# Router logits of a mixture of experts: four token tiles at once on TensorE's four column groups

## The chip, the core and the metric

The kernel runs on one core of one Trainium2 chip. The metric is the device time of one execution in microseconds (us). The engines named below are TensorE (PE; PEld is its weight load), VectorE (DVE), ScalarE (ACT), GpSimd (POOL) and SyncE (SP, which here only issues DMAs).

## The reference, cut to what matters

Two layers on 2048 tokens of 512 features. The first is a long convolution (an attention without softmax): products of keys and values are convolved with a kernel per head group and combined with the normalised queries. The second is a mixture of 16 experts. The change touches the second layer's router: logits of each token for 16 experts, and the choice of the four largest.

```python
x = x + xattn(ctx_2048, ctx_2048, layernorm(x), ssm_kernel, D, 8)
h = layernorm(x)                                # (T, 512), T = 2048
scores = softmax(h @ gate_w.T)                  # gate_w (16, 512)
topk_w, topk_i = top_k(scores, 4)
topk_w = topk_w / (topk_w.sum(-1) + 1e-20)
# each expert takes its first 256 tokens, in order of token
eout = (silu(xg @ w_gate) * (xg @ w_up)) @ w_down * weight
out = x + scatter_add(eout) + (silu(h @ sw_gate) * (h @ sw_up)) @ sw_down
```

All of it is in float32; one float32 matmul instruction of the program appears in the trace as two passes of TensorE, each a weight load and a MATMUL (a transpose appears as one).

## The kernel before

The 2048 tokens are 16 tiles of 128. The order of the instructions on every engine is the order in which the program issues them[...].

**The loop of the first layer** (line 645, 16 rounds, in the order 1, 0, 2, 3, ... of `seq`) computes one token tile of the convolution in a round. A round has four calls of `attend` (line 441), two for each of its two heads: TensorE convolves into `y` (lines 455 to 476; in all but the first ones a part `shared` comes first, which ScalarE copies to `again`), VectorE combines `y` with the queries through `z` (lines 478 to 504) into `f` (line 505), and GpSimd adds up `f` into `oT` (lines 506 to 509). `y` has two buffers. GpSimd makes the products `kv` for the next tile (line 425).

**Work of the second layer lies between.** When a tile is done, `add_to_x` (line 512) transposes it and adds it to `xs`; its statistics and normalisation run on ScalarE and GpSimd, and the transposed tile `xnT` comes either through DRAM (`send_blocks`, `fetch_blocks`, and a transpose in 32x32 blocks on VectorE, line 391) or, for the first and last tiles, through TensorE and a copy of ScalarE (line 721). Most tiles are ready two rounds after their convolution (`ready(n - 2)`, line 713, just before the fourth `attend`), the first and last one round after (line 723).

`ready` (line 629) calls `by_feature` (line 536): four matmuls with `xnT[:, c, n, :]` (128x128) as stationary and `gwT[:, c, :]` (128x16) as moving operand give `lg`, 128 tokens by 16 experts; VectorE copies it to `logits` and chooses (lines 543 to 552): the eight largest (`tops`), a memset of places 4 to 7, a match-and-replace into `rest`, and `sel`, one where an expert is chosen. `count` (line 637) adds `sel` on GpSimd to the running number `early`. `gwT` is made once, in round 0 (lines 693 to 696).

`ready` also appends a generator of the shared expert (`shared_block`, line 129) to the list `behind`; `fill(n)` (line 618) issues its next n pieces. These pieces are matmuls `sgt`, `sgu` and `so` that stand between the parts of the convolution.

**Buffers of the accumulator memory.** The pool `ps_tr` holds two buffers under the one tag `pt`. They go in turn to the transposes of `transpose_in` and `add_to_x`, to `shared`, to `lg`, and to `pg`: each new one waits until the one before the last has been read.

**After the loop** (lines 734 to 745) the last tile goes the same way, with `fill` between. Then positions within each expert's list are computed from `sel` and `early` (line 777), `compare` and `find` (lines 807 and 818) make the token lists of the experts, and the expert loop (line 979) gathers, computes and adds by DMA.

**Constants.** `masks` (line 188) makes index tables on GpSimd and VectorE in rounds 6 to 8; `exch` (line 261) is a 128x128 table that `begin` (line 288) uses in round 0 and nothing uses later.

Of the kernel before, what the change touches and what calls it, by code (L numbers as in the profile page):

```python
# [52 lines left out]
def ssm_attention__then__moe_kernel(  # L53
# [22 lines left out]
    nc = tc.nc  # L76
# [4 lines left out]
    const = ctx.enter_context(tc.tile_pool(name="const", bufs=1))  # L81
# [16 lines left out]

    xs = keep.tile([P, NT, L], F32, name="xs")
    xnT = keep.tile([P, NC, NT, P], F32, name="xnT")  # L100
    gwT = keep.tile([P, NC, E], F32, name="gwT")
    logits = keep.tile([P, NT, E], F32, name="logits")
    tops = keep.tile([P, NT, 8], F32, name="tops")
    sel = keep.tile([P, NT, E], BF16, name="sel")
# [83 lines left out]
    def masks():  # L188

        col_i = const.tile([P, R, B], I32, name="col_i")
        col_b = const.tile([P, P], F32, name="col_b")
        par_i = const.tile([P, 1], I32, name="par_i")
        bat_i = const.tile([P, 1], I32, name="bat_i")
        row_i = const.tile([P, 1], I32, name="row_i")
        par_b = const.tile([P, 1], F32, name="par_b")
        nc.gpsimd.iota(col_i, pattern=[[0, R], [1, B]], base=0, channel_multiplier=0)
        nc.gpsimd.iota(par_i, pattern=[[0, 1]], base=0, channel_multiplier=1)  # L200
        slot_i = const.tile([P, P], I32, name="slot_i")
        slot_f = const.tile([P, P], F32, name="slot_f")
        nc.gpsimd.iota(slot_i, pattern=[[1, P]], base=0, channel_multiplier=0)
        nc.gpsimd.tensor_copy(slot_f, slot_i)

        tok_i = const.tile([P, NT, 3], I32, name="tok_i")
        tok_f = const.tile([P, NT, 3], F32, name="tok_f")
        tok = const.tile([P, NT, 3], BF16, name="tok")
        row_f = const.tile([P, 1], F32, name="row_f")
        nc.gpsimd.memset(tok_i, 1)  # L210
        nc.gpsimd.iota(tok_i[:, :, 1], pattern=[[R, NT]], base=0, channel_multiplier=0)

        empty_i = const.tile([P, NSL], I32, name="empty_i")
        empty = const.tile([P, NSL], F32, name="empty")
# [27 lines left out]
        masked.update(tri=tri, tri_b=tri_b, same_b=same_b, slot_f=slot_f, tok=tok, empty=empty)  # L242
        yield
# [3 lines left out]
    with ExitStack() as att:  # L247
# [141 lines left out]
        def transpose_blocks(dst, got):  # L389

            nc.vector.transpose(dst, got.rearrange("p j (c f) -> p c j f", f=BK))
# [141 lines left out]
        def store(n, xn):  # L533
            nc.sync.dma_start(out=by_tile(xw_d[0:T, 0:L])[n], in_=xn)

        def by_feature(n):

            lg = ps_tr.tile([P, E], F32, name="lg", tag="pt")
            for c in range(NC):
                nc.tensor.matmul(  # L540
                    lg, lhsT=xnT[:, c, n, :], rhs=gwT[:, c, :], start=(c == 0), stop=(c == NC - 1)
                )
            nc.vector.tensor_copy(logits[:, n, :], lg)

            top = tops[:, n, :]
            nc.vector.max(out=top, in_=logits[:, n, :])
            nc.vector.memset(tops[:, n, K:8], 3.0e38)
            rest = small.tile([P, E], F32, name="rest")
            nc.vector.match_replace(
                out=rest, in_to_replace=top, in_values=logits[:, n, :], imm_value=-3.0e38  # L550
            )
            nc.vector.tensor_tensor(sel[:, n, :], rest, logits[:, n, :], ALU.is_lt)

        toeps = {}

# [72 lines left out]

        def ready(n):

            by_feature(seq[n])
            for t in range(2) if n == 1 else range(n, n + (n > 0)):
                count(t)
            if n < 4 or n + 1 == sum(blocks_left[0]):
                behind.append(shared_block(*blocks_left.pop(0)))

        def count(t):

            nc.gpsimd.tensor_add(early[:, t + 1, :], early[:, t, :], sel[:, t, :])

        nc.gpsimd.memset(early[:, 0, :], 0.0)
        making = masks()
# [2 lines left out]
        for n in range(NT):  # L645
# [16 lines left out]
                kvs.append(products(t * HT + 1, 1, k2))  # L662
            if n - 2 in MILD:
                transpose_blocks(xnT[:, :, n - 2, :], got_x)
            if more and not swift and n:
                qn = load.tile([P, L], F32, name="qn", tag="kn")
                stats = statistics(qn, xs[:, seq[n + 1], :])
# [24 lines left out]
            if n == 0:  # L692
                pg = ps_tr.tile([P, NC, P], F32, name="pg", tag="pt")
                for c in range(NC):
                    nc.tensor.transpose(pg[:, c, 0:E], gw[:, c * P : (c + 1) * P], ident[:E, :E])
                nc.scalar.copy(gwT, pg[:, :, 0:E])
            fill(2)
            if n > 0:
                normalise(xn, xs[:, seq[n - 1], :], *xstats)
# [13 lines left out]
                ready(n - 2)  # L713

            attend(t * HT + 1, 1, 2, tps[1], kvs[1], q2, oT)
            if n == 0:
                windows()
            if n - 1 in MILD:
# [323 lines left out]
```

## Time and profile before

| | us |
|---|---|
| three runs | 702.88, 705.42, 707.62; median 705.42 |
| the profiled execution, its own time | 702.86 |
| its span, from first to last instruction | 701.1 |
| TensorE busy / weight load busy | 675.0 (96%) / 510.0 (73%) |
| VectorE / ScalarE / GpSimd busy | 365.1 / 196.1 / 305.8 |
| logit matmuls, line 540: MATMUL / LDWEIGHTS | 15.5 / 16.7 in 128 passes |

The start takes until about 41 us, the loop of the first layer until about 348, the tail, the rest of the shared expert and the lists until about 430, the experts until about 686; the last additions to the output end the span.

How to read the profile's views. A row of the page over 40 slices gives the busy share in tenths for each 17.5 us. The view by windows gives busy time and, in brackets, the number of instructions of each engine in a stretch. The timeline lists one engine's instructions in order of time: start, duration, line, operation, tiles (out<-in), shapes, count; in square brackets the idle time ahead of it and what ended it. The chain of waits is followed back from the last instruction: at each step to what released it, or to the instruction before it on its engine. Durations of a pass are longer than the distance between passes, because passes overlap; the distance is what counts.

### The profile page before, as it was taken

Reading aid. Unit: us, or ns where it says so; the run is one execution under the profiler, and the core shown is the slowest. Engines: PE = TensorE matmul, PEld = TensorE weight load, DVE = VectorE, ACT = ScalarE, POOL = GpSimd, SP = SyncE. Lnnn points to the kernel's source line nnn. Section 1 sums busy time; section 2 is a strip of 40 time slices with the busy share of each in tenths; the row PEclk is TensorE's granted clock in tenths of the full one; section 3 lists DMA queues with packets and bytes.
Section 4 is the critical chain, followed back from the end, with each engine's and each line's share of the span. In section 5 each row is a group of like instructions: output and inputs, shape, how many; then the busy total and the mean of one; then the engine's idle time right before and its main releaser. Section 6 shows DMA issues by size and latency. Waiting matters only on the chain.

```text
span 701.1 us, 9862 instructions
## 1 busy us (share of the span) xinstructions
PE 675.0 (96%) x3437; PEld 510.0 (73%) x3437; DVE 365.1 (52%) x845; ACT 196.1 (28%) x501; POOL 305.8 (44%) x478
## 2 busy tenths in 40 slices
PE   6889999899999999999999999999999999999994
PEld 5677887777877877877868686777777777777772
DVE  4946666778968677675635311333333344333221
ACT  3443423444342343421212011122221111221220
POOL 6666646777765576545200200222233333222221
PEclk9999999999999999999999999999999999999998
DMA  6783546656566646441028301677776777777632
GB/s 156 233 238 91 137 129 148 176 135 165 146 158 172 166 105 151 123 117 45 16 90 265 88 12 34 184 211 208 202 200 186 199 199 206 203 194 194 186 46 30
DMA packets 90929, 104.17 MB, mean 149 GB/s; under 512 B 10416, under 2 KB 63504, under 8 KB 90880
## 3 DMA queue, kind: packets, MB, share of 16 engines
q1 hardware_dynamic: 83424, 86.24, 43.9%
q0 software_dynamic: 7168, 17.04, 11.6%
q8 instruction: 27, 0.44, 0.3%
q10 hardware_dynamic: 288, 0.26, 0.2%
q14 instruction: 22, 0.18, 0.1%
HBM read 75.86 MB, written 27.66 MB: 148 GB/s over the span
## 4 chain that ended last, share of the span: by engine, by line
PE 90%; DMA 5%; DVE 2%; issue 1%; SPq 1%; ACT 0%; POOLq 0%; ACTq 0%; DVEq 0%
PE sgu L155 20%; PE y L455 16%; PE pgu L918 16%; PE eo L960 12%; PE so L172 12%; PE pgu L938 4%; PE pt L126 2%; PE pgu L930 2%; PE shared L455 2%; PE sgt L141 2%; PE lg L540 1%; DMA swt<-in_L_ffn_sw_up 1%; DMA got<-sent 1%; PE ip L823 1%; PE pt L516 1%
## 5 line engine op out<-in xcount | busy, mean ns | idle before, releaser
L455 PE MATMUL y<-kv,toep 128*128 128x288 f32 x528 | 138.6, 407 | 2.7 <-DVE f L505 1.9
L455 PEld LDWEIGHTS y<-kv,toep 128*128 128x128 f32 x528 | 99.1, 190 | 33.1 <-issue 6.3
L918 PE MATMUL pgu<-xgT,w 128*128 128x256 f32 (+1 forms) x544 | 113.8, 367 | 0.8 <-ACT xgT L890 0.8
L918 PEld LDWEIGHTS pgu<-xgT,w 128*128 128x128 f32 x544 | 98.6, 190 | 20.4 <-issue 7.7
L969 POOL DMA_INDIRECT out<-eo_sb,idx x32 | 51.1, 1596 | 107.4 <-DMA out<-eo_sb,idx 71.7
L877 POOL DMA_INDIRECT g<-xw_d,idx x32 | 32.0, 1001 | 139.7 <-PE eo L960 60.4
L507 POOL TENSOR_TENSOR f<-f 128x256 f32<-128x256 f32 x60 | 43.7, 729 | 98.7 <-DVE f L505 93.3
L960 PE MATMUL eo<-wd,mid 128*128 128x512 f32 (+1 forms) x192 | 86.4, 598 | 0.0
L432 POOL TENSOR_TENSOR kv<-k 128x256 f32<-128x256 f32 x128 | 86.1, 704 | 0.0
L155 PE MATMUL sgu<-xnT,swg 128*128 128x256 f32 (+1 forms) x400 | 78.1, 338 | 1.8 <-DVE tail L149 1.8
L155 PE MATMUL sgu<-xnT,swu 128*128 128x256 f32 (+1 forms) x400 | 77.8, 337 | 0.0
L172 PE MATMUL so<-swd,smid 128*128 128x512 f32 x160 | 74.4, 594 | 0.0
L155 PEld LDWEIGHTS sgu<-xnT,swg 128*128 128x128 f32 x400 | 65.3, 191 | 9.1 <-DVE tail L149 2.0
L155 PEld LDWEIGHTS sgu<-xnT,swu 128*128 128x128 f32 x400 | 64.7, 191 | 6.3
L960 PEld LDWEIGHTS eo<-wd,mid 128*128 128x128 f32 (+1 forms) x192 | 35.1, 190 | 37.9 <-issue 33.6
L925 ACT ACTIVATE eact<-pgu 128x256 f32<-128x256 f32 (+1 forms) x34 | 12.6, 372 | 152.0 <-PE pgu L918 152.0
L172 PEld LDWEIGHTS so<-swd,smid 128*128 128x128 f32 x160 | 29.7, 190 | 31.0 <-issue 29.4
L164 ACT ACTIVATE act<-sgu 128x256 f32<-128x256 f32 (+1 forms) x50 | 17.1, 341 | 122.1 <-PE sgu L155 122.1
L926 DVE TENSOR_TENSOR mid<-eact,pgu 128x256 f32<-128x256 f32 (+1 forms) x34 | 13.8, 405 | 70.8 <-ACT eact L925 70.8
L478 DVE TENSOR_TENSOR y<-y,again 128x576 f32<-128x576 f32 x28 | 21.4, 766 | 53.1 <-PE y L455 50.3
L968 DVE TENSOR_SCALAR eo_sb<-eo,g 128x512 f32<-128x512 f32 x32 | 24.0, 750 | 46.3 <-PE eo L960 46.3
L505 DVE TENSOR_TENSOR f<-y,z 128x512 f32<-128x512 f32 x64 | 44.3, 692 | 6.2
(164 smaller groups left out, 859.0 us busy)
## 6 DMA issues: line engine op xcount, KB each, us to landing
w<-in_L_ffn_w_gate SPq DMA_DIRECT2D x16, 704.0 KB, 4.4
w<-in_L_ffn_w_up SPq DMA_DIRECT2D x16, 704.0 KB
got<-sent SPq DMA_DIRECT2D x36, 256.0 KB, 6.2
toep<-win_d SPq DMA_DIRECT2D x28, 320.0 KB, 5.2
wd<-in_L_ffn_w_down SPq DMA_DIRECT2D x16, 512.0 KB, 5.0
xs<-in_x SPq DMA_DIRECT2D x16, 256.0 KB, 5.8
kn<-in_ctx SPq DMA_DIRECT2D x16, 256.0 KB, 6.2
xw_d<-xn SPq DMA_DIRECT2D x16, 256.0 KB, 2.9
```

The costliest lines, as they stand in the source:

```text
L155: nc.tensor.matmul(pgu[:, k, :], lhsT=sw[:, c, f * P : (f + 1) * P], rhs=toks[:, c, :], start=(c == 0), stop=(c == NC - 1),)
L172: nc.tensor.matmul(po, lhsT=m[:, i * P : (i + 1) * P], rhs=swd[:, (f - 1) % (NF + 1), :], start=(f == 0), stop=(f == NF),)
L432: nc.gpsimd.tensor_mul(kv[:, c, 0 : ND * HB].rearrange("p (d w) -> p d w", d=ND), kh[:, c, 0:HB].unsqueeze(1).broadcast_to([P, ND, HB]), v ...
L455: nc.tensor.matmul(out, lhsT=toep[:, m * P : (m + 1) * P], rhs=rhs, start=(n == 0), stop=(n == len(pairs) - 1),)
L505: nc.vector.tensor_add(f, yd, z[:, :, :, BACK : BACK + HB])
L507: adder.tensor_add(f[:, :, 0:2, :], f[:, :, 0:2, :], f[:, :, 2:4, :])
L877: nc.gpsimd.indirect_dma_start(out=g, out_offset=None, in_=xw_d[:, :], in_offset=bass.IndirectOffsetOnAxis(ap=idx[:, e, n : n + 1], axis=0),)
L918: nc.tensor.matmul(pgu[:, k, cols], lhsT=w[:, k, c, f * P : (f + 1) * P], rhs=xgT[:, c, cols], start=(c == 0), stop=(c == NC - 1),)
L938: nc.tensor.matmul(pgu[:, 0, cols], lhsT=wt[:, c, 0:P], rhs=xgT[:, c, cols], start=(c == 0), stop=(c == NC - 1),)
L960: nc.tensor.matmul(po, lhsT=mid[:m, f, n * P : (n + 1) * P], rhs=wd[:m, f, :], start=(f == 0), stop=(f == NI - 1),)
L968: nc.vector.tensor_scalar_mul(o, po, g[:, L + e : L + e + 1])
L969: nc.gpsimd.indirect_dma_start(out=out, out_offset=bass.IndirectOffsetOnAxis(ap=idx[:, e, n : n + 1], axis=0), in_=o, in_offset=None, comp ...
```

## The change

The logits of four tiles are computed together, when the last of the four is ready (after tiles 3, 7, 11, and after tile 14 for three tiles; tile 15 alone as before). Operands are exchanged: the stationary operand is now `gwT`, 32 columns wide, of which 16 hold the gate's weights and 16 are zero; the moving operand is `xnT`. Each tile's result goes to its own 32 partitions of the one buffer `lq`[...]: the result is expert by token. ScalarE copies `lq` into `exch`, whose old content is no longer needed. After the fourth `attend` of that round, `turn_logits` transposes the copy by TensorE in one piece (`lt`), and VectorE copies 16 of every 32 columns to `logits`. `choose` then handles one tile each time it is called, twice a round: after the first `attend` and at the round's end. Its operations are the old ones, and the addition to `early` is now among them.

`gwT` is wider and is cleared once by GpSimd at the start. In `masks`, `slot_i` takes the memory of `col_i`, and two index operations change places for that.

```diff
-    gwT = keep.tile([P, NC, E], F32, name="gwT")
+    gwT = keep.tile([P, NC, BK], F32, name="gwT")
+    nc.gpsimd.memset(gwT, 0.0)
...
-        nc.gpsimd.iota(col_i, pattern=[[0, R], [1, B]], base=0, channel_multiplier=0)
         nc.gpsimd.iota(par_i, pattern=[[0, 1]], base=0, channel_multiplier=1)
-        slot_i = const.tile([P, P], I32, name="slot_i")
+        slot_i = col_i.rearrange("p r b -> p (r b)")
...
         nc.gpsimd.tensor_copy(slot_f, slot_i)
+        nc.gpsimd.iota(col_i, pattern=[[0, R], [1, B]], base=0, channel_multiplier=0)
...
-        def by_feature(n):
+        def logits_of(tiles):
+            g = len(tiles)
+            if g == 1:
...
+                nc.vector.tensor_copy(logits[:, n, :], lg)
+                return
+            lq = ps_tr.tile([P, P], F32, name="lq", tag="pt")
             for c in range(NC):
+                for i, n in enumerate(tiles):
+                    nc.tensor.matmul(
+                        lq[i * BK : (i + 1) * BK, :],
+                        lhsT=gwT[:, c, :],
+                        rhs=xnT[:, c, n, :],
+                        start=(c == 0),
+                        stop=(c == NC - 1),
+                    )
+            by_expert = exch
+            nc.scalar.copy(by_expert[0 : g * BK], lq[0 : g * BK])
+            by_expert_of.append((tiles, by_expert))
+
+        def turn_logits():
+            if not by_expert_of:
+                return
+            tiles, by_expert = by_expert_of.pop()
+            g = len(tiles)
+            lt = ps_tr.tile([P, P], F32, name="lt", tag="pt")
+            nc.tensor.transpose(
+                lt[:, 0 : g * BK], by_expert[0 : g * BK], ident[0 : g * BK, 0 : g * BK]
+            )
+            nc.vector.tensor_copy(
+                logits[:, tiles[0] : tiles[0] + g, :],
+                lt[:, 0 : g * BK].rearrange("p (g e) -> p g e", e=BK)[:, :, 0:E],
+            )
+            unchosen.extend(tiles)
+
+        def choose(count=1):
+            for n in unchosen[:count]:
...
+                nc.vector.tensor_tensor(sel[:, n, :], rest, logits[:, n, :], ALU.is_lt)
+                nc.gpsimd.tensor_add(early[:, n + 1, :], early[:, n, :], sel[:, n, :])
+            del unchosen[:count]
...
         def ready(n):
-            by_feature(seq[n])
-            for t in range(2) if n == 1 else range(n, n + (n > 0)):
-                count(t)
+            if n % 4 == 3 or n == NT - 2:
+                logits_of(list(range(n // 4 * 4, n + 1)))
...
             if n - 2 in MILD:
                 transpose_blocks(xnT[:, :, n - 2, :], got_x)
+            choose()
...
             attend(t * HT + 1, 1, 2, tps[1], kvs[1], q2, oT)
+            turn_logits()
...
             if n in (6, 7, 8):
                 next(making)
+            choose()
...
-        fill(2)
+        fill(1)
+        turn_logits()
+        choose(NT)
+        fill(1)
         normalise(xn, xs[:, NT - 1, :], *xstats)
...
-        by_feature(NT - 1)
-        count(NT - 1)
+        logits_of([NT - 1])
+        unchosen.append(NT - 1)
+        choose(NT)
```

More of the change, by code (lines that the diff above doesn't have):

```diff
@@ L534, in store @@
             nc.sync.dma_start(out=by_tile(xw_d[0:T, 0:L])[n], in_=xn)
-        def by_feature(n):
-            lg = ps_tr.tile([P, E], F32, name="lg", tag="pt")
-            for c in range(NC):
-                nc.tensor.matmul(
-                    lg, lhsT=xnT[:, c, n, :], rhs=gwT[:, c, :], start=(c == 0), stop=(c == NC - 1)
-                )
[L543 to L552, printed above, removed]
+        def logits_of(tiles):
+            g = len(tiles)
+            if g == 1:
+                n = tiles[0]
+                lg = ps_tr.tile([P, E], F32, name="lg", tag="pt")
+                for c in range(NC):
+                    nc.tensor.matmul(
+                        lg,
+                        lhsT=xnT[:, c, n, :],
+                        rhs=gwT[:, c, 0:E],
+                        start=(c == 0),
[4 more added lines that the diff above has]
+            lq = ps_tr.tile([P, P], F32, name="lq", tag="pt")
+            for c in range(NC):
+                for i, n in enumerate(tiles):
+                    nc.tensor.matmul(
+                        lq[i * BK : (i + 1) * BK, :],
+                        lhsT=gwT[:, c, :],
+                        rhs=xnT[:, c, n, :],
+                        start=(c == 0),
+                        stop=(c == NC - 1),
+                    )
+            by_expert = exch
+            nc.scalar.copy(by_expert[0 : g * BK], lq[0 : g * BK])
+            by_expert_of.append((tiles, by_expert))
@@ new lines, in ssm_attention__then__moe_kernel @@
+        by_expert_of = []
+        def turn_logits():
[10 more added lines that the diff above has]
+                lt[:, 0 : g * BK].rearrange("p (g e) -> p g e", e=BK)[:, :, 0:E],
+            )
+            unchosen.extend(tiles)
@@ new lines, in ssm_attention__then__moe_kernel @@
+        unchosen = []
+        def choose(count=1):
+            for n in unchosen[:count]:
+                top = tops[:, n, :]
+                nc.vector.max(out=top, in_=logits[:, n, :])
+                nc.vector.memset(tops[:, n, K:8], 3.0e38)
+                rest = small.tile([P, E], F32, name="rest")
+                nc.vector.match_replace(
+                    out=rest, in_to_replace=top, in_values=logits[:, n, :], imm_value=-3.0e38
+                )
+                nc.vector.tensor_tensor(sel[:, n, :], rest, logits[:, n, :], ALU.is_lt)
+                nc.gpsimd.tensor_add(early[:, n + 1, :], early[:, n, :], sel[:, n, :])
+            del unchosen[:count]
@@ L629, in ready @@
         def ready(n):
-            by_feature(seq[n])
-            for t in range(2) if n == 1 else range(n, n + (n > 0)):
-                count(t)
+            if n % 4 == 3 or n == NT - 2:
+                logits_of(list(range(n // 4 * 4, n + 1)))
             if n < 4 or n + 1 == sum(blocks_left[0]):
                 behind.append(shared_block(*blocks_left.pop(0)))
-        def count(t):
-            nc.gpsimd.tensor_add(early[:, t + 1, :], early[:, t, :], sel[:, t, :])
         nc.gpsimd.memset(early[:, 0, :], 0.0)
@@ L695, in ssm_attention__then__moe_kernel @@
                     nc.tensor.transpose(pg[:, c, 0:E], gw[:, c * P : (c + 1) * P], ident[:E, :E])
-                nc.scalar.copy(gwT, pg[:, :, 0:E])
+                nc.scalar.copy(gwT[:, :, 0:E], pg[:, :, 0:E])
             fill(2)
```

## The prediction, made before the changed kernel ran

> **What bounds the kernel now.** I first read the busy row of TensorE over the 40 slices, then the busy time by stage, then the chain of waits, then single instructions around every logit matmul.
>
> ```profile
> PE   6889999899999999999999999999999999999994
> ```
>
> ```profile
> core 0: us, PE busy (x) PEld busy (x) DVE busy (x) ACT busy (x) POOL busy (x), PEclk, DMA share, GB/s
> 41.00:116.00 75.00, 75.00 (x448) 61.06 (x448) 48.17 (x116) 28.79 (x80) 45.87 (x82) 1.00 0.51 131
> 116.00:133.00 17.00, 14.56 (x76) 11.37 (x74) 12.38 (x30) 6.45 (x16) 11.21 (x21) 1.00 0.67 166
> 133.00:165.00 32.00, 30.45 (x163) 24.14 (x164) 24.73 (x59) 11.98 (x34) 21.96 (x47) 1.00 0.69 172
> 165.00:348.00 183.00, 183.00 (x797) 141.70 (x796) 131.68 (x314) 64.60 (x163) 111.73 (x200) 1.00 0.49 122
> ```
>
> From 41 to 348 us TensorE hardly ever idles; VectorE is at 72% (131.68 of 183) and GpSimd at 61%. The chain of waits is 90% TensorE. So TensorE time taken out of this stretch comes off the end, except in two short places, which these rows of TensorE's timeline show (the bracket is the idle time before the row and who ended it):
>
> ```profile
> 133.17 1.05 PE L155 MATMUL sgu<-xnT,swg 128*128 128x128 f32 x7 [1.84 <-DVE tail L149]
> ...
> 162.77 0.75 PE L455 MATMUL shared<-kv,toep 128*128 128x288 f32 x2 [1.37 <-DVE xs L518]
> ```
>
> There VectorE is behind. A third place is the first logit matmul, at 38.0: what follows it waits until 40.76 for the transfer of `swt`, so taking it away frees nothing.
>
> The price of one tile's logits, from the chain:
>
> ```profile
> 62.18 1.72 PE so L172 x4
> 63.90 0.80 PE lg L540 x8
> 64.69 1.81 PE so L172 x4
> ```
>
> Four float32 matmuls are eight passes. They last 0.80 us, 0.10 a pass, although each moves only 16 columns: what takes the time is loading 128 weight columns (`xnT`) eight times. The four `so` passes after it take 1.81 instead of 1.72, so one tile costs **0.89 us** of TensorE.
>
> [...] The kernel already has a row to hold against this, the 64-column matmuls of the experts, line 930:
>
> ```profile
> 435.63 1.03 PE L918 MATMUL pgu<-xgT,w 128*128 128x256 f32 x4
> 436.58 1.09 PE L930 MATMUL pgu<-xgT,wt 128*64 128x128 f32 x16
> 437.61 1.99 PE L938 MATMUL pgu<-xgT,wt 128*128 128x256 f32 x8
> 439.44 0.27 PE L126 MATMUL pt<-ident,g 128*128 128x128 f32 x1
> ...
> 678.35 1.09 PE L930 MATMUL pgu<-xgT,wt 128*64 128x128 f32 x8
> 679.37 1.16 PE L938 MATMUL pgu<-xgT,wt 128*128 128x128 f32 x8
> ```
>
> Sixteen passes on two groups take 1.03 us start to start (436.58 to 437.61); eight passes on one group, at 678.35, take 1.02. The second group is free[...]. Four groups no row shows.
>
> **The change, part by part.**
>
> *Removed.* Fifteen of the sixteen logit blocks (tile 15 keeps its own). Tile 1's, at 38.0, is hidden. Tiles 3, 7, 11 and 14 are where the groups of four, four, four and three now stand. Nine blocks simply vanish from a busy TensorE (tiles 0, 2, 4, 6, 8, 9, 10, 12, 13): 9 x 0.89 = **-8.0 us**. Tile 5's, at 160.4, stands before the 1.37 us wait above. `lg` used to take one of the two `pt` buffers, so `shared` had to wait until VectorE had read the one before (`xs`, 162.7). Without `lg` that wait goes, but `y` behind it still needs its own buffer, released by the `f` of VectorE that ends at 162.12. So `y` starts at about 162.15 instead of 163.36: **-1.2 us**, not 0.89 + 1.37.
>
> *Added on TensorE.* A group of four is 16 matmuls, 32 passes of 32 weight columns and 128 moving columns. The nearest row is L930: eight slots of 0.11 us (four transposes of line 516, which also move 128 columns, take 0.44 in the chain), plus its entry and exit. The block runs 1.03; the four L918 before it take 0.95 (435.63 to 436.58) where their pass of 0.216 would give 0.86, so +0.09; the eight L938 after it take 1.83 to the next row where 8 x 0.216 is 1.73, so +0.10. Together 1.22. With all four groups at once `lq` also needs eight slots: I take **1.22 us**. The transpose `lt` is one pass, 0.11 (four of line 516 take 0.44). At tiles 7, 11 and 14 the price is 1.22 + 0.11 - 0.89 = 0.44 each: **+1.3 us**. Bounds for the unknown: two groups at a time is sixteen slots, 2.1 us; one at a time 32 slots, 3.8 us. Below 1.22 I see nothing, since eight slots on one group cost that.
>
> *The handshake.* `lt` reads what ScalarE copies from `lq`[...]. Between them stand `shared` (0.49) and ten passes `y` (2.42), 2.91 us. On ScalarE the copy (about 0.28, as the 128x128 activation of line 164 takes) stands after the copy of `kp`. At tile 7 `kp` ends at 208.72 and TensorE would reach `lt` at about 207.5 + 2.9 = 210.4: covered by 1.4 us. At tile 11 `kp` ends at 296.5, cover 2.1 us. At tile 14 two more blocks of matmuls lie between. At tile 3 it is not covered:
>
> ```profile
> 128.25 0.41 ACT L397 COPY q<-q 128x256 f32<-128x256 f32 x1 [0.57 <-DVE q L391]
> 128.56 0.61 ACT L710 COPY kp<-kn 128x512 f32<-128x512 f32 x1
> 129.08 0.39 ACT L473 COPY again<-shared 128x288 f32<-128x288 f32 x1
> ```
>
> TensorE reaches `lt` at about 126.0, the copy ends near 129.4. TensorE then still has `sgt`, six `y` and 16 `sgu` to do before the `sgu` that it now starts at 133.17: 0.9 + 1.5 + 1.8 from 129.5 is 133.8. On VectorE `again` comes 0.28 later, and the new copy of `lt` (0.2) stands ahead of `tail`: 133.6. So the place ends some **+0.6 us** later, and the 0.89 saved there is lost, because it was hidden. The late transfer `got` (lands 124.47) that makes this place follows a wait on TensorE (`toep` free at 115.87), so it moves up with the tiles saved before.
>
> *Added on ScalarE:* four copies of 0.28, at 35% busy; they also delay `again`, which VectorE needs, by 0.28. Four tiles' `f` are done 3 us or more before TensorE needs the buffer from 190 us on, so that is free; from 150 to 180 only 1.2 to 2 us, and no group stands there.
>
> *Moved on VectorE.* The five small operations of choosing (0.8 us a tile: 362.17 to 362.95 for tile 15) now stand after the end of an attention block instead of before `y,again`. At 133.6 they come before `z` of the next tile, which runs 1.5 us later; TensorE meets that again at the `sgu` of 138.4, which waits for `smid`, almost exactly in time: 0 to 0.4 us, within my range. Twelve copies `logits` go, four of up to 64 columns come. In the tail three tiles' choices and a copy (2.6 us) fall into VectorE's idle 4.75 us before 361.16; tile 15's choice is as before. GpSimd's additions `early` stay sixteen, each behind an `f` and before the next, which waits for VectorE anyway; in the tail they stand after `rstd`.
>
> *At nothing.* The memset of `gwT` lies in GpSimd's idle 3.9 us before 6.57. Reordering of the iotas moves about 0.1 us on GpSimd in its slack. No transfer is added or moved; SP's queue keeps its order. The experts from 430 us are TensorE's throughout and only start earlier.
>
> **Sum:** -8.0 - 1.2 + 1.3 + 0.6 = **-7.3 us** against the profiled execution's own 702.86 (span 701.1), so 695.6. The median of the three runs is 705.42, 0.36% higher; scaled, **698.1 us**, 1.04% less.
>
> **Rivals.**
> - *Two groups at a time.* For it: no row shows more than two[...]. Against: L930's second group is entirely free. Price: +0.87 at tiles 7 and 11, +0.44 at 14, near nothing at 3: -5.1 us, **700.3**. One at a time would cost +2.6, +2.6, +1.7 and perhaps 1 at tile 3: +0.6, **706**.
> - *Slower: the handshake stalls TensorE at each group*, as it must at tile 3. Place: `lt` after tiles 7, 11, 14. Price: tile 3's 3.4 us at each, 10.2 us: +2.9, **708.3**. It decides once the copy ends more than 2.9 us after `lq`, and the whole change loses once the three waits add up to over 7.3 us. Against it: the covers of 1.4 and 2.1 us above.
> - *VectorE or the fetches take over as pace.* TensorE's saving in the steady stretch is absorbed, and half is left: **701.5**. For it: VectorE waits for `got` seven times (5.7 us in all). Against: 28% idle VectorE and 3 us of slack.
>
> **How the numbers follow.** All four groups at once 0.62 (698.1); two at a time 0.17 (700.3); one at a time 0.05 (706); handshake 0.06 (708.3); pace elsewhere 0.10 (701.5). The three runs before spread over 4.7 us, so about 1% is what can be told from no change; the likeliest case sits on that border. Its runs put about six tenths of it on the faster side and next to nothing of the others: faster 0.41, within 1% 0.52, slower 0.07. The range 695.3 to 703.5 takes in the bounds of the matmuls' overlap down to two groups and leaves out the last rivals and the noise beyond.
>
> **What would show it.** Right: `lq` 32 passes in 1.0 us start to start; no idle before `lt` but at tile 3, there some 3.4 us; the 1.37 us before `shared` gone; expert stage starting some 7 us earlier. Wrong: `lq` at 2 us or more, idle time before `lt` at 210 or 299, new waits of TensorE for `f` or `smid`.

## The result, and the profile after

The changed kernel takes **700.09 us** (median of 12 runs, 697.82 to 701.93), the kernel before 706.06 (12 runs, 702.88 to 710.1): a ratio of 0.9915, 95% interval 0.9892 to 0.9939. That is 6.0 us less, 4.3 to 7.6 by the interval; the prediction's sum was 7.3 for the profiled execution. The profiled execution took 697.82 us, against 702.86 of before.

The changed kernel's page, the rows that answer to those of before:

```profile
span 696.1 us, 9866 instructions
PE 668.5 (96%) x3441; PEld 500.4 (72%) x3441; DVE 363.4 (52%) x834; ACT 197.7 (28%) x505; POOL 305.9 (44%) x479
...
PE   6889999798999999999999999999999999999994
```

TensorE is busy for 6.5 us less than the 675.0 of before, the span is 5.0 shorter. Two digits of the row are one lower: the 7 in the eighth slice (about 122 to 139 us), which holds tile 3's place, and the 8 in the tenth (157 to 174 us), which holds tile 5's. The view by windows, cut three microseconds later at tile 3's place than the prediction's:

```profile
core 0: us, PE busy (x) PEld busy (x) DVE busy (x) ACT busy (x) POOL busy (x), PEclk, DMA share, GB/s
116.00:136.00 20.00, 15.97 (x107) 12.37 (x106) 15.37 (x39) 6.76 (x18) 12.86 (x23) 0.91 0.69 167
136.00:165.00 29.00, 27.20 (x134) 20.55 (x133) 22.17 (x58) 11.62 (x33) 19.03 (x43) 1.00 0.63 159
165.00:348.00 183.00, 182.81 (x832) 139.32 (x832) 130.46 (x304) 65.99 (x167) 112.91 (x201) 1.00 0.48 122
```

In the first stretch TensorE idles 4.03 us (the same 116 to 136 us of before: 2.61), and its granted clock is 0.91 on average, where it was 1.00. From 165 on it still hardly idles.

What was least certain, four column groups at once (a group here: the 32 partitions of `lq` that one tile's result fills, from a stationary operand of 32 columns), is seen in the groups of TensorE with shapes kept apart (columns: mean ns of one pass, then idle before) and in the timeline at tile 7:

```profile
L558 PE MATMUL lq<-xnT,gwT 128*32 128x128 f32 x120 | 4.3, 276 | 0.0
L578 PE MATMUL lt<-ident,exch 128*128 128x128 f32 x3 | 0.9, 291 | 4.0 <-ACT exch L566 4.0
```

```profile
204.89 1.08 PE L558 MATMUL lq<-xnT,gwT 128*32 128x128 f32 x32
205.91 0.75 PE L457 MATMUL shared<-kv,toep 128*128 128x288 f32 x2
206.49 2.59 PE L457 MATMUL y<-kv,toep 128*128 128x288 f32 x10
208.92 0.27 PE L578 MATMUL lt<-ident,exch 128*128 128x128 f32 x1
```

Thirty-two passes take 1.02 us from their start to that of `shared`; the eight passes on one group of 64 columns, at 678.35 in the kernel before, take the same 1.02. No idle time stands ahead of `lt` here. All of its 4.0 us belongs to tile 3.

**A table of stretches** compares the runs. Cuts are the starts of the blocks of transposes of `oT` on TensorE (`pt<-ident,oT`; the second is number 1). Stretch 1-4 holds the places of tiles 0 and 2, 4-5 that of tile 3, 5-6 tile 4, 6-7 tile 5, 7-15 tiles 6 to 14; the last two columns are the flight of the transfer `got` on which tile 3's place waits (from its issue to its landing) and the time from cut 1 to the start of the last matmul. What lies ahead of cut 1 (48.6 to 52.4 us) varies from run to run and is left out. From cut 15 to the end the runs differ by about 0.1 us.

| run | 1-4 | 4-5 | 5-6 | 6-7 | 7-15 | flight of `got` | cut 1 to end |
|---|---|---|---|---|---|---|---|
| before | 68.92 | 19.36 | 20.57 | 16.79 | 177.87 | 6.32 | 641.07 |
| e9, before | 68.92 | 19.41 | 20.57 | 16.79 | 177.87 | 6.63 | 641.13 |
| e10, before | 68.92 | 21.51 | 20.57 | 18.48 | 177.87 | 6.85 | 644.92 |
| after | 67.13 | 22.59 | 19.68 | 16.39 | 174.09 | 7.50 | 637.55 |
| e11, after | 67.13 | 23.81 | 19.68 | 16.39 | 174.07 | 7.54 | 638.75 |
| e1 | 67.13 | 21.01 | 19.68 | 16.62 | 173.81 | 7.77 | 635.93 |
| e2 | 67.13 | 23.55 | 19.68 | 16.46 | 173.67 | 7.87 | 638.17 |
| e3 | 67.13 | 22.02 | 19.68 | 16.37 | 173.67 | 7.33 | 636.55 |
| e4 | 67.13 | 22.93 | 19.68 | 16.39 | 177.74 | 7.71 | 641.54 |
| e5 | 67.13 | 21.18 | 19.68 | 16.39 | 174.07 | 7.66 | 636.13 |
| e6 | 67.13 | 20.66 | 19.68 | 16.39 | 186.74 | 7.31 | 648.16 |
| e7 | 67.13 | 21.36 | 19.68 | 16.41 | 174.01 | 8.06 | 636.27 |
| e8 | 68.92 | 22.10 | 19.68 | 16.31 | 173.67 | 6.76 | 638.38 |

Most stretches repeat to a few hundredths. Stretch 4-5 does not, and it is where the change lost 3.2 us in the first pair of profiles.

### The profile page after: what moved, and what is told of

Same layout as the page of the kernel before. It is cut to its first block, busy times and chain, and to the rows that moved or that the text cites. A ratio compares the mean times of both kernels' runs of the same rounds, so it can differ in the third digit from the quotient of the medians.

```text
span 696.1 us, 9866 instructions
## 1 busy us (share of the span) xinstructions
PE 668.5 (96%) x3441; PEld 500.4 (72%) x3441; DVE 363.4 (52%) x834; ACT 197.7 (28%) x505; POOL 305.9 (44%) x479
## 4 chain that ended last, share of the span: by engine, by line
PE 88%; DMA 4%; DVE 4%; POOL 2%; issue 1%; ACT 1%; SPq 0%; POOLq 0%; ACTq 0%; DVEq 0%
PE sgu L157 20%; PE pgu L970 16%; PE y L457 14%; PE eo L1012 12%; PE so L174 11%; PE pgu L990 4%; PE pt L128 2%; PE pgu L982 2%; PE sgt L143 2%; PE shared L457 2%; DMA got<-sent 1%; PE ip L875 1%; PE pt L518 1%; POOL kv L434 1%; DVE y L506 1%
## 5 line engine op out<-in xcount | busy, mean ns | idle before, releaser
L977 ACT ACTIVATE eact<-pgu 128x256 f32<-128x256 f32 (+1 forms) x34 | 12.7, 372 | 152.0 <-PE pgu L970 152.0
```

## The experiments

**e4: is it the order of the loops that lets four groups overlap?** The matmuls are issued tile by tile instead of chunk by chunk.

```diff
-            for c in range(NC):
-                for i, n in enumerate(tiles):
+            for i, n in enumerate(tiles):
+                for c in range(NC):
```

> The two loops of the group's matmuls are exchanged: all four chunks of a tile on its column group, then the next tile. Theory N (only matmuls that stand next to each other on different column groups overlap): nearly serial, lq lasts 3.5 us instead of 0.81, +2.6, +2.6, +1.7 us at tiles 7, 11, 14 and nothing at tile 3, 707 us. Rival Q[...]: lq stays 0.8 us, 700 us.

A single run, 702.53 us. TensorE's timeline of e4 at tile 7:

```profile
205.77 2.46 PE L558 MATMUL lq<-xnT,gwT 128*32 128x128 f32 x32
208.16 0.75 PE L457 MATMUL shared<-kv,toep 128*128 128x288 f32 x2
```

The block takes 2.39 us instead of 1.02, and that lies between the two theories (3.5 and 0.8). By the starts of single passes, the first four and the last four come about 0.11 us apart, alone, and between them passes start in pairs, within 0.03 us of each other. Read off this pattern, groups work at once only where one tile's last passes meet the next tile's first. In the change's order, at the same tile, four passes start within 0.02 us of each other, and the next four 0.11 us later. The price of the other order is 177.74 - 174.09 = 3.7 us of stretch 7-15, nearly all that this stretch had gained (177.87 before). In these two orders, the groups overlap where passes of different groups stand next to each other in the queue: 1.02 us with neighbours on different groups, 2.39 with eight passes of one group in a row.

By the same reading, a tile's first pass starts 0.47 us after the first of the tile ahead, whose eight passes take 0.79 us from first to last start: ahead of that tile's last passes, although it stands behind them in the program. Neither is shown directly, since the records do not name a pass's tile.

**e6: is it the grouping or the exchanged operands?** The four tiles are computed together, but with `xnT` as stationary operand as before, tile by tile; ScalarE's copy and `lt` are gone, since nothing has to be turned.

```diff
-            lq = ps_tr.tile([P, P], F32, name="lq", tag="pt")
-            for c in range(NC):
-                for i, n in enumerate(tiles):
+            lq = ps_tr.tile([P, g, E], F32, name="lq", tag="pt")
+            for i, n in enumerate(tiles):
+                for c in range(NC):
                     nc.tensor.matmul(
+                        lq[:, i, :],
+                        lhsT=xnT[:, c, n, :],
+                        rhs=gwT[:, c, 0:E],
...
+            nc.vector.tensor_copy(logits[:, tiles[0] : tiles[0] + g, :], by_expert)
```

> Grouping and later choices as in the changed kernel, but the operands as before the change: xnT stationary, four tiles' logits one after the other into one buffer, which VectorE copies; no ScalarE copy and no lt. Theory M (the gain comes from the four column groups working at once): the group lasts 3.2 us instead of 0.81, +2.0, +2.0, +1.2 at tiles 7, 11, 14; at tile 3, where the handshake is gone, -2 us: 703 us. Rival: the gain comes from moving the choices and from the buffers of ps_tr, and the operands do not matter: 698 us.

707.42 us (12 runs), ratio 1.0026 (0.9994 to 1.0057): grouping alone gains nothing measurable. The trace shows more than the price of the passes. TensorE's timeline of e6 at tile 7, and its windows (columns as above):

```profile
205.01 4.57 PE L558 MATMUL lq<-gwT,xnT 128*128 128x16 f32 x32
209.42 1.31 PE L457 MATMUL shared<-kv,toep 128*128 128x288 f32 x2
210.52 4.47 PE L457 MATMUL y<-kv,toep 128*128 128x288 f32 x10
```

```profile
205.00:207.00 2.00, 2.00 (x20) 1.99 (x18) 1.90 (x4) 1.15 (x3) 2.00 (x4) 1.00 0.00 0
207.00:209.00 2.00, 2.00 (x14) 2.00 (x13) 0.31 (x1) 0.93 (x2) 1.92 (x4) 0.62 0.49 126
209.00:211.00 2.00, 2.00 (x6) 1.57 (x7) 0.00 (x0) 0.23 (x1) 2.00 (x4) 0.50 0.91 264
211.00:213.00 2.00, 2.00 (x6) 1.43 (x5) 0.00 (x0) 1.94 (x6) 1.70 (x3) 0.50 0.66 134
```

TensorE is busy in every window by its records, yet the granted clock falls to 0.50, and the ten `y` passes take 4.3 us (210.52 to 214.83) instead of the 2.4 of 206.49 to 208.92 in the changed kernel. The rounds of tiles 7 and 11 last 28.11 and 28.18 us, against 22.52 and 22.58 in the changed kernel. The same passes of 16 columns, 0.8 us at a time, lowered no clock in the profile of before: it is 1.00 there from 41 us to 686. The exchange of the operands, with the copy and `lt` that come with it, is thus worth 186.74 - 174.09 = 12.7 us of stretch 7-15. Tile 14's round, in which the clock stays at 1.00, is 1.5 us longer with its 24 passes; eight more passes at the 0.112 us from start to start that the trace shows at full clock make that 2.4 at tiles 7 and 11. So the passes themselves come to 6.2 us, by this estimate, and the clock to the other 6.5: about half each.

**e1: the wait at tile 3.** In the changed kernel TensorE's timeline there reads:

```profile
120.42 0.75 PE L457 MATMUL shared<-kv,toep 128*128 128x288 f32 x2
121.01 2.59 PE L457 MATMUL y<-kv,toep 128*128 128x288 f32 x10
127.63 0.33 PE L578 MATMUL lt<-ident,exch 128*128 128x128 f32 x1 [4.03 <-ACT exch L566]
127.80 1.59 PE L143 MATMUL sgt<-xnT,swt 128*128 128x128 f32 x8
129.18 2.80 PE L457 MATMUL y<-kv,toep 128*128 128x288 f32 x6
131.81 1.05 PE L157 MATMUL sgu<-xnT,swg 128*128 128x128 f32 x8
```

The chain of waits says why `lt` is late: the fetch `got`, then VectorE, then ScalarE with `kp` ahead of the copy.

```profile
115.22 7.50 DMA got<-sent
...
122.74 0.71 DVE k L393
...
126.89 0.52 ACT kp L756
127.41 0.17 ACT exch L566
...
127.63 0.33 PE lt L578
```

And the windows of the changed kernel show what follows the idle time:

```profile
126.00:128.00 2.00, 0.37 (x3) 0.37 (x4) 0.54 (x2) 1.39 (x4) 2.00 (x4) 1.00 0.84 209
128.00:130.00 2.00, 2.00 (x10) 1.85 (x9) 1.93 (x5) 0.54 (x3) 1.92 (x5) 0.54 0.70 143
130.00:132.00 2.00, 2.00 (x7) 1.39 (x6) 1.76 (x8) 0.73 (x1) 2.00 (x4) 0.61 0.62 165
```

The granted clock is 0.54 and 0.61 in these two windows: by the changes of the clock that the trace keeps, it is half from 128.14 to 131.56, for 3.41 us. The six `y` take 2.63 us to the next row. Before they took 1.53, from the first to the second of these rows of before:

```profile
127.85 1.69 PE L455 MATMUL y<-kv,toep 128*128 128x288 f32 x6 [0.77 <-DVE f L505]
129.38 1.05 PE L155 MATMUL sgu<-xnT,swg 128*128 128x128 f32 x8
```

So 3.41 us of half speed follow a wait of 4.03 us, and begin 0.5 us after its end; what can be said of the moment from all profiles stands under "When the clock falls", below. The wait holds up what stands behind `lt` as well: `sgt`, which does not read `lt`, starts 0.17 us after it. e1 moves `lt` behind the next round's first `attend`:

```diff
                 transpose_blocks(xnT[:, :, n - 2, :], got_x)
+            turn_logits()
             choose()
...
             attend(t * HT + 1, 1, 2, tps[1], kvs[1], q2, oT)
-            turn_logits()
```

> turn_logits moves from the end of the round to behind the first attend of the next round; everything else as in the changed kernel. Theory H (the transpose lt blocks TensorE at tile 3 until ScalarE's copy comes, 4.0 us idle, after which the granted clock is low): the idle time before lt shrinks to under 0.5 us, the y passes behind it go back from 0.48 to 0.24 us, the sgu that waits for tail starts about 2 us earlier, 698.0 us in all against 700.1. Rival V (VectorE, late by the transfer got, paces this place whatever TensorE does): the idle time moves to another instruction, 0 to -0.6 us in all.

697.78 us (6 runs), ratio 0.9889 (0.9865 to 0.9913); stretch 4-5 falls to 21.01. TensorE's timeline of e1:

```profile
125.46 1.05 PE L143 MATMUL sgt<-xnT,swt 128*128 128x128 f32 x8
128.45 3.10 PE L457 MATMUL y<-kv,toep 128*128 128x288 f32 x6 [1.94 <-DVE f L507]
131.34 0.42 PE L578 MATMUL lt<-ident,exch 128*128 128x128 f32 x1
...
133.94 1.16 PE L157 MATMUL sgu<-xnT,swg 128*128 128x128 f32 x8 [0.22 <-DVE tail L151]
```

`sgt` no longer stands behind the copy: it starts straight behind the ten `y`, at 125.46. The wait for `f` is still there, the clock falls here too (0.50 from 130 to 132 us; `y` takes 2.89 us), but VectorE's `tail` sets the end of this place, so the slow passes only fill what was a wait of 1.84 us before. Rival V was thus right about what paces the place once `lt` is out of the way, and the stretch is still 1.6 us shorter than in the profile of the changed kernel.

**e5: the clock's share.** `lt` stays; in the wait TensorE turns the unit matrix 36 times, and nothing reads the result.

```diff
+            if n == 5:
+                busy = ps_mm.tile([P, P], F32, name="busy", tag="mm")
+                for i in range(36):
+                    nc.tensor.transpose(busy, ident, ident)
             turn_logits()
```

> The changed kernel, with 36 transposes of a constant (3.9 us of TensorE) put into the wait before lt of tile 3; their result is read by nothing. lt must wait for ScalarE's copy as before. Theory K (the 4 us of idle TensorE let its granted clock fall, and the next passes pay for it): sgt and y behind lt run at the full clock, 0.24 instead of 0.48 us a pass of y, the stretch from the transposes of oT at 115.7 to those at 138.3 (22.6 us) shrinks by 1.7 us, 698.4 in all. Rival: the slow passes only fill time in which VectorE is late anyway: the stretch stays 22.6, 700 us.

697.23 us (4 runs), ratio 0.9876 (0.9829 to 0.9924). TensorE's timeline of e5:

```profile
124.67 4.09 PE L765 MATMUL busy<-ident 128*128 128x128 f32 x36
129.12 0.33 PE L578 MATMUL lt<-ident,exch 128*128 128x128 f32 x1 [0.36 <-ACT exch L566]
129.29 1.06 PE L143 MATMUL sgt<-xnT,swt 128*128 128x128 f32 x8
130.18 1.62 PE L457 MATMUL y<-kv,toep 128*128 128x288 f32 x6
```

`lt` comes as late as before (8.5 us after the start of `lq`, against 8.2), but the clock stays at 1.00, `sgt` takes 0.89 to the next row instead of 1.38 and `y` 1.46 instead of 2.63. Useless work shortens the stretch by 1.41 us. Among the experiments this is the plainest: `lt` waits as long as before, and only the idleness is gone. All four of its runs have a mean granted clock of 0.994 or 0.995; the changed kernel's twelve have 0.987 to 0.994.

**e7: both.** `lt` moved as in e1, and 18 such transposes where it was.

> As e1_turn_later, with 18 transposes of a constant (2.0 us) behind the fourth attend of round 5, where TensorE idled 2.1 us before y and the clock then fell for six passes. Theory K: those passes back at 0.24 us, -1.4 us against e1, 696.4. Rival: VectorE's tail sets the next sgu anyway: no change, 697.8.

699.8 us (7 runs), ratio 0.9904 (0.987 to 0.9939); stretch 4-5 is 21.36. The two cures don't add up: with full clock (1.00 in every window from 116 to 142 us) TensorE waits 1.84 us for `tail` again, as before the change. That the median is 2.0 us above e1's is not explained; the intervals of the two overlap.

**e2 and e3: do the moved choices hold VectorE up?** e2 lets the two calls act only from round 8 on; e3 adds e1's move.

```diff
-            choose()
+            if n >= 8:
+                choose()
```

> choose is called only from round 8 on, so that no choice of tiles 0 to 3 stands on VectorE between 150 and 160 us. Theory C (two choices of 0.8 us each in a chain of VectorE operations that already paces TensorE there make it wait 1.8 us for f at y): that wait shrinks to under 0.5 us, -1.5 us in all, 698.6. Rival: the wait is there without choices, as 1.4 us stood near this place before the change: 0 to -0.3 us.

> Both edits: turn_logits behind the next round's first attend, choices from round 8. If H and C hold and are independent: -3.5 us, 696.6. If both places hang on the late transfer got: under -1 us.

701.21 us (12 runs, ratio 0.9935, 0.9915 to 0.9955) and 699.15 (6 runs, 0.9912, 0.9888 to 0.9936). Stretch 6-7, tile 5's place, stays at 16.46 and 16.37, as the rival said: the wait for `f` that theory C names only shrinks, from 1.80 to 1.18 us, and the next `y` then waits 0.46 us, so holding the choices off gives this place nothing. Stretch 7-15 falls from 174.09 to 173.67, all of it in tile 6's round: they do cost 0.4 there. In e3 stretch 4-5 is 22.02, 1.0 above e1. e3's timeline shows the clock falling later than in e1:

```profile
131.08 0.33 PE L578 MATMUL lt<-ident,exch 128*128 128x128 f32 x1
...
135.04 1.92 PE L157 MATMUL sgu<-xnT,swg 128*128 128x128 f32 x8 [1.84 <-DVE tail L151]
136.74 1.92 PE L157 MATMUL sgu<-xnT,swu 128*128 128x128 f32 x8
```

Here the half speed (a granted clock of 0.50 from 136 to 138 us) hits the `sgu` behind the wait for `tail` (1.70 us from row to row instead of 0.89), where nothing hides it. The same waits, a different moment, another 1.6 us.

**e8: without a group at tile 3.** Tiles 0 to 3 keep the old form; groups start with tile 4.

```diff
-            if n % 4 == 3 or n == NT - 2:
+            if n < 4:
+                logits_of([seq[n]])
+                unchosen.append(seq[n])
+                if n:
+                    unchosen.sort()
+                    choose(4)
+            elif n % 4 == 3 or n == NT - 2:
...
-            choose()
+            if n >= 6:
+                choose()
```

> Tiles 0 to 3 one by one as before the change (logits and choice at once), groups of four from tile 4 on. Theory H (tile 3's group loses 3.2 us by its handshake and the clock): the stretch around tile 3 is as long as before the change; 1.8 us of tiles 0 and 2 are given back, 3.2 are won: -1.4 us against the changed kernel, 698.7. Rival V (the place is as slow without the group, by the late transfer): +1.8 us, 701.9.

699.48 us (9 runs), ratio 0.9902 (0.9872 to 0.9933). Stretch 4-5 is 22.10, not the 19.4 of before, though neither `lt` nor `lq` is there. Two things account for it. `got` was issued 0.2 us after cut 4 instead of 0.5 before it, behind a row of issues on SyncE's queue, and half speed (0.50 from 138 to 140 us) hits the `sgu` behind the wait for `tail`, as in e3. So in this profile the place loses nearly as much without the handshake.

**e9, e10, e11: how steady is stretch 4-5?** The kernel before twice more, the changed one once more.

> The kernel before, profiled once more. In its first profile the stretch from the transposes of oT at 118.6 us to those at 138.0 took 19.36 us and the transfer got reached VectorE 5.9 us after its start; in all eight profiles of changed versions, the one without a group at tile 3 (e8) included, got came 6.8 to 7.7 us after it and the stretch took 20.7 to 23.6. Theory R (the transfer's arrival varies from run to run, and the first profile of before was a lucky one): got at over 6.5, the stretch 20.5 to 22. Theory S (the change delays it): 5.9 and 19.4 again.

> As e9_before_again, a third profile of the kernel before: R says again over 6.5 and 20.5 to 22 us, or a value between; S says 5.9 and 19.4.

> The changed kernel, profiled once more. Theory H (the handshake and the clock belong to the change): TensorE idles 4 us or more before lt at tile 3 again, slow passes of y behind it, the stretch 22 to 23.5 us. Rival: the idle time was chance; under 2 us, and the stretch is near that of the kernel before in the same job.

A single run each: 705.08, 708.4 and 703.01 us. Before gives 19.36, 19.41, and once 21.51; `got` reaches VectorE 5.9 and 6.4 us after cut 4 in e9 and e10, not over 6.5 as theory R had it. In e10 the clock falls behind the wait for `tail` (0.57 from 136 to 140 us), and again at tile 5 (0.70 from 168 to 172 us; the stretch is 18.48 instead of 16.79):

```profile
135.33 1.23 PE L155 MATMUL sgu<-xnT,swg 128*128 128x128 f32 x8 [1.85 <-DVE tail L149]
```

The changed kernel gives 22.59 and 23.81. The kernel before thus has the same weakness, but escapes it here in two profiles of three; behind the longer idle wait ahead of `lt` (3.0 to 4.5 us) the clock fell in all four profiles that have it (after, e11, e2, e4).

**When the clock falls.** In each of the 13 profiles, all changes of the granted clock lie whole multiples of 3.413 us apart; in the profile of after, half clock begins at 128.144, ends at 131.557 (one multiple later) and begins again at 691.343, behind the last matmul (164 more). Call each such stretch of 3.413 us a window. To compare windows, count the columns that TensorE's passes move in them, each pass taken as lasting its columns at 1.2 per ns (the 288 of `y` in 0.24 us). At full clock, up to the last matmul, all 20 windows with at most 1,527 columns were followed by half clock, and none of the 2,545 with 1,536 or more. (In the profile of before the lowest of the windows has 1,536; in that of after the lowest two have 529 and 1,536.) Some of them:

| run | window, us | idle in it, us | columns | the next window |
|---|---|---|---|---|
| before | 131.47 to 134.88 | 1.70 | 1,847 | full clock |
| e10, before | 132.87 to 136.29 | 1.85 | 1,495 | half |
| after | 124.73 to 128.14 | 2.90 | 529 | half |
| e5 | 126.09 to 129.51 | 0.36 | 3,322 | full clock |
| e6 | 204.08 to 207.49 | 0.00 | 1,472 | half |

In these profiles, whether a wait of this length was followed by half clock goes with where the windows lie: e10's wait of 1.85 us lies whole in one window, while the wait of 1.84 us in the profile of before is cut by a border, at 131.47. The count fits e6 too, which slows down without idling: its passes move 16 columns each, and the window ahead of the fall holds 1,472. This border between 1,527 and 1,536 columns was read off these same profiles, and no run was made to test it; moving the windows by 0.1 us against the record already mixes a few cases at the border.

**Stretch 4-5 taken apart.** VectorE's first work on `got` starts 5.88 us after cut 4 in the profile of before; call d what it is later in another run. Take 19.36 + d from each stretch. What is left:

| run | d | left | half clock in or around the stretch |
|---|---|---|---|
| e9 | 0.05 | 0.0 | none |
| e7 | 1.83 | 0.2 | none |
| e1 | 1.48 | 0.2 | 3.41 us, hidden by the wait for `tail` |
| e6 | 1.01 | 0.3 | 3.41 us, hidden by the same waits |
| e5, waits for `lt` | 1.41 | 0.4 | none |
| e8 | 1.11 | 1.6 | 3.41 us |
| e10 | 0.50 | 1.7 | 3.41 us |
| e3 | 0.87 | 1.8 | 3.41 us |
| after, waits for `lt` | 1.15 | 2.1 | 3.41 us |
| e4, waits for `lt` | 1.50 | 2.1 | 3.41 us |
| e2, waits for `lt` | 1.61 | 2.6 | 6.83 us |
| e11, waits for `lt` | 1.12 | 3.3 | 6.83 us |

Work of 3.41 us at half speed, a granted clock of 0.50, can lose 1.7 us (an estimate: half of 3.41), and that is the step between the rows. So of the 3.2 us lost in the profile of after, about 1.2 is `got` landing later, 0.4 the handshake itself (e5), and the remaining 1.7 the clock. That the parts add up is arithmetic over single profiles, not a run that isolates each.

Why `got` lands later is open. In the four profiles with a stretch 1-4 of 68.92 its flight is 6.3 to 6.9 us, in the nine with 67.13 it is 7.3 to 8.1. While it flies in the changed kernel the DMA engines are full:

```profile
115.00:117.00 2.00, 2.00 (x10) 1.32 (x9) 0.99 (x3) 0.00 (x0) 0.06 (x1) 1.00 0.99 161
117.00:119.00 2.00, 2.00 (x8) 1.30 (x7) 1.86 (x5) 0.00 (x0) 0.00 (x0) 1.00 1.01 244
119.00:121.00 2.00, 2.00 (x36) 1.32 (x36) 1.48 (x4) 1.02 (x3) 1.20 (x2) 1.00 1.06 261
```

The kernel before had 0.78, 0.96 and 0.83 in the windows 118 to 120, 120 to 122 and 122 to 125. Rounds that are 1.8 us shorter in sum bring the same transfers closer together; this fits all thirteen profiles, and none isolates it.

## Why the prediction was right, and where it wasn't

The time fell within the range, and the likeliest case, all four groups at once, is what happened. The number alone would not have said so: 700.09 lies nearest to the 700.3 of the rival with two groups at a time, and the fall of 6.0 us between that rival's 5.1 and the 7.3 forecast. It is the timeline of `lq` that decides. The terms against the traces, before and after:

| term | predicted | measured |
|---|---|---|
| nine blocks that vanish | -8.0 | -7.6 |
| tile 5's place | -1.2 | -0.4 |
| groups at tiles 7, 11, 14 | +1.3 | +1.2 |
| tile 3's place | +0.6 | +3.2 |
| the tail, from cut 15 to the first `eo` | 0 | +0.1 |
| sum | -7.3 | -3.5 |

- **The vanished blocks.** Each gives 0.89 to 0.90 us (stretch 5-6; rounds 22.15 to 21.26). Tile 6 gives only 0.48: two transposes of `oT` wait for GpSimd, the only new wait of the stretch, and e2 shows that the moved choices cause it (with them held off, that round too is 21.26). The prediction had looked for the choices' cost at tile 3 alone.
- **The price of `lq`.** The 0.43 measured at tile 7 (22.09 to 22.52) and at tile 11 is the predicted 0.44; at tile 14 it is 0.31. Taken from the experts' rows of two groups, 1.22 + 0.11 - 0.89 was right, and the covers of 1.4 and 2.1 us before `lt` held. That loading 128 columns is what paced the old passes fits the trace of before: the first two passes of the block at 63.7 start 0.03 us apart, the others 0.11 us, as far apart as their weight loads (0.11 us too). That two free groups mean four was an estimate from the row of line 930; the trace of `lq` shows it. The rivals of two groups at a time and of a stall at every group fell. (The third rival's 701.5 is a slip: half of 7.3 us, scaled in the same way, gives 701.8.) At tile 7 the 32 passes start within 0.81 us, the old block's eight within 0.70: about four times as dense. e4 shows where something like the first rival is true: in the other order of loops, where at most two passes start together and the block takes 2.39 us.
- **Tile 5's place.** The wait for the buffer of `shared` went as forecast. But `y` behind it then waits 1.80 us for `f`, one of the prediction's own signs of being wrong:

```profile
159.87 0.65 PE L457 MATMUL shared<-kv,toep 128*128 128x288 f32 x2
162.32 2.66 PE L457 MATMUL y<-kv,toep 128*128 128x288 f32 x10 [1.80 <-DVE f L507]
```

  The prediction held `f` still at its old time, 162.12, and `shared` ahead of it starts 2.9 us earlier than before (159.87, not 162.77); in the changed kernel `f` also comes at about 162.2, behind choices that VectorE now does at 157.5 to 158.4. e2, without these choices, shows what lies under them; its chain of waits to the next `y`:

```profile
159.28 0.60 DVE xnT L393
159.87 6.42 DMA got<-sent
...
166.31 0.71 DVE k L393
...
168.72 0.70 DVE f L507
...
169.67 1.69 PE y L457 x6
```

  VectorE's transpose `xnT` comes first, only then is the next fetch issued, and the next `f` waits for it. Time taken from TensorE here returns as waiting for VectorE and the fetch: the third rival, in one place.
- **Tile 3's place**, the term that failed. The text has "0.9 + 1.5 + 1.8 from 129.5 is 133.8": durations of a TensorE at full clock, behind a wait of 3.4 us, and a fetch that keeps its flight of 6.3. The handshake alone comes to 0.4, near the forecast of 0.6; the clock adds about 1.7 and the later fetch about 1.2 in the profile of after. The profile of before had no sign of the first (its clock is 1.00 through this place).
- **The sum and the medians.** By the first two profiles the terms give 3.5 us, by the means of three and two profiles (642.4 and 638.2) 4.2. The profiled executions differ by 5.0: cut 1 comes 1.1 us earlier, which is within its own spread, and the end after the last matmul is 0.4 shorter. The expert stage (its first `eo`) starts 4.6 us earlier and not the forecast 7. The medians differ by 6.0, because the profiled execution of before lies further below its median (3.2 us) than that of the changed kernel (2.3). The profiled execution of before has a mean granted clock of 0.995, while 42 other runs of it, timed beside e1 to e8, average 0.990; those at 0.993 or more took 701.56 to 706.17 us, those at 0.988 or less 705.79 to 709.58. The changed kernel's twelve runs average 0.991, against 0.994 in its profile. So most executions of the kernel before lose time to the clock as well, and on average about as much. The first pair of profiles probably makes the change's loss at tile 3 look larger than it usually is; where in the kernel the clock fell, these averages do not say. That the total came so near to the forecast is in part luck: it rests on a clock that the prediction left out on both sides.

By their medians e5 (697.23) and e1 (697.78) are the fastest, 2 to 3 us under the changed kernel. But their intervals against the kernel before overlap with that of the changed kernel and with each other, so neither the gain nor which is better is settled.

## What to carry to other kernels

A wait of TensorE can cost more than its length, as here, where a granted clock of 0.50 for 3.41 or 6.83 us followed all four waits of 3.0 to 4.5 us for `lt`, and filling the wait gave back 1.41 us (e5). When an edit lengthens a wait of 2 us to 4, price such work at half speed too, and see whether a later wait hides it, as in e1. Compare profiles only after a look at the mean granted clock of each, and of the other runs: one undisturbed profile of a kernel is no measure of it. Work with 32 stationary columns is worth issuing so that neighbours in the queue use different column groups: the same sixteen matmuls took 1.02 us so and 2.39 in the other order, which lost 3.7 of the 3.8 us that stretch 7-15 had gained. And a stage of which one engine is relieved can return part of the gain where another engine, or a fetch that is issued only after that engine's work, becomes the pace, as at tile 5's place (0.4 us of the 1.2 forecast).

## What the runs showed of the hardware that was not expected

- Four column groups of 32 work fully at once in float32: 32 passes in 1.02 us at tile 7, no longer than eight on one group (1.02, line 930 before), four starts within 0.02 us of each other and the next four 0.11 us later. Ordered by group they take 2.39 us (e4).
- The changes of the granted clock lie multiples of 3.413 us apart (half clock from 128.144 to 131.557 in the profile of after). Of such windows at full clock, the 20 in which TensorE moved at most 1,527 columns were followed by half clock, the 2,545 with 1,536 or more were not (counted from the 13 profiles, not tested by a run of its own).
- The granted clock fell without any idle time in the records in e6: it goes to 0.62 and then 0.50 during and after 4.4 us of passes that load 128 columns and move 16, with TensorE busy for the whole 2.00 us of each window from 203 to 219.
- The moment of the fall varies from run to run with the same program: behind waits of 1.8 to 1.9 us it came in some profiles and not in others (e9 and e10 are the same kernel, 19.41 and 21.51); behind the four idle waits of 3.0 to 4.5 us for `lt` it always came.
- The same fetch of 256 KB flies for 6.3 to 8.1 us in the same place of the program; why is open.
